# Cross attention on one core: the two big products by two levels of Winograd blocks in f32, or by three products of 12-bit parts

## The chip, the cores and the metric

The kernel runs on one core of a Trainium2 chip. The metric is the device time of one execution in microseconds, as the median of several runs. The profiled execution is one of its own; its span goes from the first to the last instruction and is a little shorter than the time of a run.

A core has five engines with a queue of instructions each, all in order: TensorE (matmuls, from SBUF into PSUM), VectorE, ScalarE, GpSimd and SyncE, which here only starts DMAs. GpSimd and ScalarE can start DMAs too. An instruction that waits holds everything behind it on its queue.

## The reference

Eight batches, 512 channels, 1024 positions. `x` are the inputs that ask, `ctx` those that are asked.

```python
q = einsum('bcn,dc->bnd', x, Wq) + bq           # 64 wide
k = einsum('bcn,dc->bdn', ctx, Wk) + bk[:, None]
v = einsum('bcn,dc->bdn', ctx, Wv) + bv[:, None]  # 512 wide
attn = softmax(einsum('bnd,bdm->bnm', q, k), axis=2)
out = einsum('bcm,bnm->bcn', v, attn) + x
```

All of it in float32. The two big products are V's (512 by 512 by 1024) and the last one (512 by 1024 by 1024).

## The kernel before, in words

A batch is done in this order: queries and keys (`project`, L181), scores in pairs of 64-row matmuls with the keys as columns on the partitions (`scores`, L223), the maximum over the keys (`fold`, `highest`; a reduction over partitions on GpSimd, L253), the exponentials E in place (`lower`, `exponential`), their sums (`total`, L258) and reciprocals. It never forms V. It takes Y = ctx E first and then Wv Y, so that Wv meets a matrix that is already summed, and divides Y by the sums in between (`scale_y`).

Both products go by Winograd's form of Strassen's scheme: a 2 by 2 block product with seven multiplications, and sums of blocks on both sides. In the first product the inputs' blocks `a` come from `x2T`, a transposed copy, and four of their sums (`S1` to `S4`) are made by VectorE, ScalarE and accumulating DMAs; the sums of E's blocks (`T1` to `T4`) by VectorE, ScalarE and DMAs. `multiply` (L375) does one of the seven products as two banks of four (first product) or two (second) matmuls 128 by 128 by 512. Five of the seven of the first product are split once more by the same scheme (`multiply_seeded`, `multiply_onto`, `inner_product` L437), with VectorE sums in `inner_left` and `inner_right`. Results are joined from PSUM by `evict_y` and `evict_o`.

The order of all engines is written out by hand (`manual_schedule`): `period` issues the instructions of a batch and, in between, scores, maxima and exponentials of the next batch and queries and keys of the one after. `head` is the special start of batch 0, with the loads of x1 and x2 in halves; the last batch adds x1 from SBUF and stores tile by tile. Elsewhere x1 is added to a result by an accumulating DMA on GpSimd's queue (L603) and the result is stored from SyncE's queue (L604).

All matmul operands are plain float32.

Of the kernel before, what the change touches and what calls it, by code (L numbers as in the profile page):

```python
# [9 lines left out]
F32 = mybir.dt.float32  # L10
AF = mybir.ActivationFunctionType
ALU = mybir.AluOpType


@with_exitstack
def kernel(
    ctx: ExitStack,
    tc: tile.TileContext,
    x1: bass.AP,
    x2: bass.AP,  # L20
    x2T: bass.AP,
# [4 lines left out]
    out: bass.AP,  # L26
):

    nc = tc.nc
    P = 128
    B, C, N = x1.shape
    D = wqk.shape[3]
    CT = C // P
    H = 512
    MH = N // P // 2  # L70
    WARM = 12
# [4 lines left out]
    dram = ctx.enter_context(  # L76
        tc.tile_pool(name="dram", bufs=2, space=bass.MemoryType.DRAM)
    )
    ps_s = ctx.enter_context(
        tc.tile_pool(name="ps_s", bufs=2, space=bass.MemoryType.PSUM)  # L80
    )
    ps_a = ctx.enter_context(
        tc.tile_pool(name="ps_a", bufs=1, space=bass.MemoryType.PSUM)
    )
# [3 lines left out]
    wq_sb, wk_sb = wqk_sb[:, 0], wqk_sb[:, 1]  # L88
    bq_sb, bk_sb = bqk_sb[:, 0:1], bqk_sb[:, 1:2]
    bv_sb = const.tile([P, CT], F32, name="bv_sb")  # L90
    w = {
        k: const.tile([P, 2, C // 2], F32, name=f"w_{k}")
        for k in ("11", "12", "21", "22", "S1", "S2", "S4")
    }

    def load_values():
        for r in range(2):
            for k in range(2):
                nc.sync.dma_start(w[f"{r + 1}{k + 1}"], wvT[r, k])

    def left_sums(a, *ks):

        for k in ks:
            if k == "S3":
                nc.vector.tensor_tensor(a["21"], a["11"], a["21"], ALU.subtract)
                a["S3"] = a["21"]
            elif k == "S4":
                nc.vector.scalar_tensor_tensor(a[k], a["12"], -1.0, a["S2"], ALU.mult, ALU.subtract)
            else:
                x, y, op = {"S1": ("21", "22", ALU.add), "S2": ("11", "S1", ALU.subtract)}[k]  # L110
                nc.vector.tensor_tensor(a[k], a[x], a[y], op)

    def value_sums(*ks):

        for k in ks:
            out, x, y, op = {
                "S1": ("S1", "21", "22", ALU.add),
                "S2": ("S2", "S1", "11", ALU.subtract),
                "S3": ("21", "11", "21", ALU.subtract),
                "S4": ("S4", "12", "S2", ALU.subtract),  # L120
            }[k]
            nc.vector.tensor_tensor(w[out], w[x], w[y], op)
        w["S3"] = w["21"]

    class Batch:
        def __init__(self, b):
            self.b = b
            self.a, self.e, self.t, self.y, self.o = {}, {}, {}, {}, {}
            self.mx, self.top, self.den, self.few, self.rden, self.row = {}, {}, {}, {}, {}, {}
            self.tmp, self.bank = {}, {}  # L130
            self.inner = {}

    def load_x(s, x):

        s.x = sb.tile([P, CT, N], F32, tag="x", name=f"x_{s.b}_{x.tensor.name}")
        for c in range(CT):
            nc.sync.dma_start(s.x[:, c, :], x[s.b, ts(c, P), :])

    def load_a(s, *ks):
        for k in ks:  # L140
            s.a[k] = sb.tile(
                [P, MH, C // 2], F32, tag=f"a{k}", name=f"a{k}_{s.b}", bufs=1 + (k[0] == "2")
            )
            nc.sync.dma_start(s.a[k], x2T[s.b, int(k[0]) - 1, int(k[1]) - 1])

    def sum_a(s, *ks):
        for k in ks:
            if k != "S3":
                s.a[k] = sb.tile([P, MH, C // 2], F32, tag=f"a{k}", name=f"a{k}_{s.b}")
        left_sums(s.a, *ks)  # L150

    def begin_s1(s):

        s.a["S1"] = sb.tile([P, MH, C // 2], F32, tag="aS1", name=f"aS1_{s.b}")
        nc.sync.dma_start(s.a["S1"], x2T[s.b, 1, 0])

    def end_s1(s):

        nc.gpsimd.dma_start(s.a["S1"], x2T[s.b, 1, 1], accum_op=ALU.add)

    def negate(s, k):

        if k == "S2":
            s.a[k] = sb.tile([P, MH, C // 2], F32, tag="aS2", name=f"aS2_{s.b}")
        else:
            s.a[k] = s.a["21"]
        nc.scalar.mul(s.a[k], s.a["S1" if k == "S2" else "21"], -1.0)

    def add_11(s, k):

        nc.gpsimd.dma_start(s.a[k], x2T[s.b, 0, 0], accum_op=ALU.add)

    def project(s, nm, w_sb, bank=None):

        if bank:
            ps = ps_a.tile([P, H], F32, tag=bank, name=f"ps_{nm}_{s.b}")
        else:
            ps = ps_s.tile([P, 2, H], F32, tag="sc", name=f"ps_{nm}_{s.b}")[:, 0, :]
        for c in range(CT):
            for h, r in ((0, lo), (1, hi)):  # L180
                nc.tensor.matmul(  # L181
                    ps[r, :],
                    w_sb[:, c, :],
                    s.x[:, c, ts(h, H)],
                    start=(c == 0),
                    stop=(c == CT - 1),
                )
        return ps

    def queries(s, bank=None):  # L190

        ps = project(s, "q", wq_sb, bank)
        s.q = sb.tile([P, N], F32, tag="q", name=f"q_{s.b}", bufs=2)
        for h, r, o in ((0, lo, hi), (1, hi, lo)):
            nc.scalar.activation(
                s.q[r, ts(h, H)], ps[r, :], AF.Identity, bias=bq_sb[r, :]
            )
        for h, r, o in ((0, lo, hi), (1, hi, lo)):
            nc.sync.dma_start(s.q[o, ts(h, H)], s.q[r, ts(h, H)])

    def keys(s, bank=None):

        ps = project(s, "k", wk_sb, bank)
        s.k = sb.tile([P, H], F32, tag="k", name=f"k_{s.b}", bufs=2)
        nc.scalar.activation(s.k, ps, AF.Identity, bias=bk_sb)

    def scores(s, h, i, bank=None):


        if i == 0:  # L210
            s.e[h] = sb.tile([P, 2, MH, H], F32, tag=f"e{h}", name=f"e_{s.b}_{h}")
        e = s.e[h]
        if bank:
            whole = None
            ps = [
                ps_a.tile([P, H], F32, tag=f"{bank}{g}", name=f"ps_s{bank}{g}_{s.b}_{h}_{i}")
                for g in range(2)
            ]
        else:
            whole = ps_s.tile([P, 2, H], F32, tag="sc", name=f"ps_s_{s.b}_{h}_{i}")  # L220
            ps = [whole[:, g, :] for g in range(2)]
        for g, r in ((0, lo), (1, hi)):
            nc.tensor.matmul(  # L223
                ps[g], s.k[r, ts(i, P)], s.q[r, ts(h, H)], start=True, stop=True
            )

        def copy():
            if bank:
                for g in range(2):
                    nc.scalar.copy(e[:, g, i, :], ps[g])  # L230
            else:
                nc.scalar.copy(e[:, :, i, :], whole)  # L232

        copy.ps = ps
        return copy

    def fold(s, h, i, kind, op):

        e = s.e[h]
        if i == 1:  # L240
            s.mx[h] = sb.tile([P, 2, H], F32, tag="fold", name=f"{kind}_{s.b}_{h}", bufs=2)
        f = s.mx[h]
        nc.vector.tensor_tensor(f, e[:, :, 0, :] if i == 1 else f, e[:, :, i, :], op)  # L243

    def fold_halves(s, h, op):
        f = s.mx[h]
        nc.vector.tensor_tensor(f[:, 0, :], f[:, 0, :], f[:, 1, :], op)

    def highest(s, h, halves=True):
        if halves:  # L250
            fold_halves(s, h, ALU.max)
        s.top[h] = sb.tile([P, H], F32, tag="top", name=f"top_{s.b}_{h}", bufs=2)
        nc.gpsimd.partition_all_reduce(s.top[h], s.mx[h][:, 0, :], P, ReduceOp.max)  # L253

    def total(s, h):
        fold_halves(s, h, ALU.add)
        s.den[h] = sb.tile([P, H], F32, tag="den", name=f"den_{s.b}_{h}", bufs=2)
        nc.gpsimd.partition_all_reduce(s.den[h], s.mx[h][:, 0, :], P, ReduceOp.add)  # L258
        s.few[h] = sb.tile([P, H // P], F32, tag="few", name=f"few_{s.b}_{h}", bufs=2)
        nc.gpsimd.dma_start(  # L260
            s.few[h], s.den[h][0:1, :].rearrange("o (p f) -> o p f", p=P)
        )

    def invert(s, h):

        nc.vector.reciprocal(s.few[h], s.few[h])  # L266
        s.row[h] = row = dram.tile([1, H], F32, tag="row", name=f"row_{s.b}_{h}")
        nc.gpsimd.dma_start(row.rearrange("o (p f) -> (o p) f", p=P), s.few[h])

    def spread(s, h):  # L270

        s.rden[h] = s.den[h]
        nc.gpsimd.dma_start(s.rden[h], s.row[h].broadcast_to([P, H]))

    def shares(s, h):
# [761 lines left out]
```

## Time and profile before

| | us |
|---|---|
| median of 3 runs | 687.22 |
| lowest, highest run | 686.67, 687.75 |
| span of the profiled execution | 685.4 |
| TensorE busy | 677.5 |
| VectorE busy | 605.9 |
| ScalarE busy | 329.0 |
| GpSimd busy | 211.4 |

How to read the lines that follow: a group of instructions has its line in the kernel, its engine (PE is TensorE's matmuls, PEld its loads of the stationary operand, DVE VectorE, ACT ScalarE, POOL GpSimd, SP SyncE; a q behind a name is the queue that starts DMAs), the operation, the tiles written and read, shape and count; then busy microseconds and the mean nanoseconds of one; then idle time in front of it and what ended it. A row of the timeline has its start, its length, and the instructions that are merged in it. Matmuls overlap in their records: the pace is the distance of starts, not the length. A DMA row ends with the KB of one and the median microseconds from issue to landing.

### The profile page before, as it was taken

What the parts mean: (1) busy time and instruction counts of PE and PEld (TensorE: products, weight loads), DVE (VectorE), ACT (ScalarE), POOL (GpSimd) and SP (SyncE); (2) the same over time, 40 slices, a digit from 0 to 9 for tenths busy, and PEclk for the clock granted to TensorE, in tenths of its full rate; (3) what the DMA queues carried; (4) which work ended last, traced back from release to release, by engine and by line L of the source; (5) the groups of instructions that cost most, each with busy time, mean ns of one, the idle gap of its engine ahead of it and who ended that gap; (6) DMA issues with size and microseconds to landing.
All of it is one profiled execution on the core that took longest, in us unless ns stands there. A gap on an engine that the chain in (4) does not pass through costs nothing.

```text
span 685.4 us, 7053 instructions
## 1 busy us (share of the span) xinstructions
PE 677.5 (99%) x2384; PEld 391.1 (57%) x2384; DVE 605.9 (88%) x744; ACT 329.0 (48%) x545; POOL 211.4 (31%) x175
## 2 busy tenths in 40 slices
PE   8999999999999999999999999999999999999997
PEld 5333554535547665566655576464854747556763
DVE  1999997987799989799979999799999979999884
ACT  2734364236355465554645637446465356553320
POOL 0125113421153411633125421344214351364100
PEclk9999999999999999999999999999999999999999
DMA  9655366836958949889598795987969881689502
GB/s 300 267 212 172 139 231 120 201 105 187 248 143 194 198 155 266 193 186 218 160 291 160 187 240 143 298 166 180 253 135 214 177 202 64 125 155 269 128 14 109
DMA packets 49620, 126.89 MB, mean 185 GB/s; under 512 B 5424, under 2 KB 7728, under 8 KB 49584
## 3 DMA queue, kind: packets, MB, share of 16 engines
q0 software_dynamic: 21456, 50.93, 42.0%
q1 hardware_dynamic: 27840, 75.11, 29.9%
q10 hardware_dynamic: 288, 0.39, 0.2%
q8 instruction: 19, 0.31, 0.2%
q14 instruction: 17, 0.14, 0.1%
HBM read 85.20 MB, written 16.81 MB: 149 GB/s over the span
## 4 chain that ended last, share of the span: by engine, by line
PE 83%; DVE 8%; DMA 6%; issue 1%; ACT 1%; SPq 1%; DVEq 0%; ACTq 0%; POOLq 0%
PE ps_ya L375 13%; PE ps_oa L375 9%; PE ps_yc L437 7%; PE ps_oc L375 7%; PE ps_ya L437 6%; PE ps_s L223 5%; PE ps_q L181 4%; PE ps_k L181 3%; PE ps_o L375 3%; PE ps_o L395 3%; PE ps_i3chain L437 3%; PE ps_i4chain L437 3%; PE ps_i7chain L437 2%; PE ps_i2chain L437 2%; DMA sum<-e 2%; PE ps_yc L375 2%
## 5 line engine op out<-in xcount | busy, mean ns | idle before, releaser
L375 PE MATMUL ps_ya<-eT,aS 128*128 128x512 f32 x192 | 84.9, 595 | 0.2 <-ACT uy L386 0.2
L258 POOL PARTITION_ALL_REDUCE den<-sum x16 | 53.5, 3345 | 96.4 <-DVE few L266 54.6
L288 DVE TENSOR_TENSOR e<-e,top 128x1024 f32<-128x1024 f32 x60 | 69.8, 1219 | 12.6 <-POOL top L253 12.6
L253 POOL PARTITION_ALL_REDUCE top<-max x16 | 38.0, 2376 | 98.5 <-DVE few L266 37.0
L292 ACT ACTIVATE e<-e 128x1024 f32<-128x1024 f32 x60 | 62.5, 1057 | 10.6 <-DVE e L288 9.1
L607 POOL DMA_DIRECT2D sum<-e x21 | 25.7, 1223 | 127.5 <-ACT sum L612 40.0
L375 PEld LDWEIGHTS ps_ya<-eT,aS 128*128 128x128 f32 x192 | 36.1, 190 | 44.8 <-issue 41.6
L375 PE MATMUL ps_oc<-yT,w 128*128 128x512 f32 x128 | 57.5, 593 | 0.5 <-DVE uo L600 0.5
L375 PE MATMUL ps_oa<-yT,w_S 128*128 128x512 f32 x128 | 57.6, 593 | 0.0
L232 ACT COPY e<-ps_s 128x1024 f32<-128x1024 f32 x46 | 45.4, 1027 | 12.5 <-PE ps_s L223 12.0
L223 PE MATMUL ps_s<-q,k 64*128 64x512 f32 x188 | 49.0, 608 | 0.8 <-ACT q L642 0.8
L386 ACT COPY uy<-ps_ya 128x512 f32<-128x512 f32 x28 | 16.0, 589 | 55.1 <-PE ps_ya L375 48.6
L375 PEld LDWEIGHTS ps_oc<-yT,w 128*128 128x128 f32 x128 | 24.2, 190 | 31.5 <-issue 29.2
L375 PEld LDWEIGHTS ps_oa<-yT,w_S 128*128 128x128 f32 x128 | 24.2, 190 | 30.8 <-issue 30.1
L243 DVE TENSOR_TENSOR max<-max,e 128x1024 f32<-128x1024 f32 x30 | 36.7, 1225 | 2.2
L386 ACT COPY uo<-ps_oa 128x512 f32<-128x512 f32 x32 | 18.7, 585 | 37.0 <-PE ps_oa L375 37.0
L223 PEld LDWEIGHTS ps_s<-q,k 64*128 64x128 f32 x188 | 17.9, 186 | 23.9 <-issue 18.3
L542 DVE TENSOR_TENSOR y<-y,den 128x1024 f32<-128x1024 f32 x24 | 29.3, 1221 | 0.3
L375 PE MATMUL ps_oa<-y,w_S 128*128 128x512 f32 (+1 forms) x68 | 28.8, 567 | 0.0
L395 PE MATMUL ps_o<-y,w 128*128 128x512 f32 x64 | 28.8, 592 | 0.0
L375 PE MATMUL ps_o<-y,w 128*128 128x512 f32 x64 | 28.8, 592 | 0.0
L551 DVE TENSOR_TENSOR y<-ps_yc,uy 128x512 f32<-128x512 f32 x40 | 25.7, 683 | 1.3 <-ACT uy L532 0.4
(200 smaller groups left out, 1475.5 us busy)
## 6 DMA issues: line engine op xcount, KB each, us to landing
x_in_x_dram<-in_x_dram SPq DMA_DIRECT2D x60, 512.0 KB, 7.6
a<-in_x2T_dram SPq DMA_DIRECT2D x32, 512.0 KB, 9.3
sum<-e POOLq DMA_DIRECT2D x21, 512.0 KB, 6.3
r<-in_x_dram POOLq DMA_DIRECT2D x14, 512.0 KB, 8.9
uo<-in_x_dram POOLq DMA_DIRECT2D x14, 512.0 KB, 8.5
out_dram<-r SPq DMA_DIRECT2D x14, 512.0 KB, 4.4
out_dram<-uo SPq DMA_DIRECT2D x14, 512.0 KB, 5.4
aS<-in_x2T_dram POOLq DMA_DIRECT2D x12, 512.0 KB, 6.4
```

Source lines behind the costliest of these rows:

```text
L181: nc.tensor.matmul(ps[r, :], w_sb[:, c, :], s.x[:, c, ts(h, H)], start=(c == 0), stop=(c == CT - 1),)
L223: nc.tensor.matmul(ps[g], s.k[r, ts(i, P)], s.q[r, ts(h, H)], start=True, stop=True)
L232: nc.scalar.copy(e[:, :, i, :], whole)
L243: nc.vector.tensor_tensor(f, e[:, :, 0, :] if i == 1 else f, e[:, :, i, :], op)
L253: nc.gpsimd.partition_all_reduce(s.top[h], s.mx[h][:, 0, :], P, ReduceOp.max)
L258: nc.gpsimd.partition_all_reduce(s.den[h], s.mx[h][:, 0, :], P, ReduceOp.add)
L288: nc.vector.tensor_tensor(e, e, top, ALU.subtract)
L292: nc.scalar.activation(e, e, AF.Exp)
L375: nc.tensor.matmul(ps[:, n], left[ka][:, k, ts(j, P)], right[kb][:, k, n], start=opens and k == 0, stop=i in (2, 3, 4) and k == n_k - 1, s ...
L386: nc.scalar.copy(s.tmp[i][:, j, :], ps)
L395: nc.tensor.matmul(ps, w["11"][:, k, ts(j, P)], s.y["11"][:, k, :], start=k == 0, stop=False, skip_group_check=True)
L437: nc.tensor.matmul(ps, s.inner[i][ka][:, k, :], s.inner[i, "t"][kb][:, k, :], start=opens and k == 0, stop=z in (2, 3, 4) and k == MH // 2 ...
```

## The change

The block scheme is gone. Every operand of the two big products is split into three parts of type float32r: `h`, the number rounded to 12 bits; `l`, the scaled or unscaled rest; `d`, a combination of both. Three matmuls (`d`, `h`, `l`) take the place of one, and the results X (from `h` and `l`) and Y (from `d`) are combined with factors of T = 4096 on the way out of PSUM.

V is now formed first, as [m, c] (`values`), with the bias already in Y's bank (`seed_y`); the last product takes E's columns as the stationary operand and V as the moving one, and gives the result as [n, c] (`results`), one tile of 128 positions by 512 channels at a time. The division by the sums has become the factor with which X and Y are taken out (`take_results`), since a position is now a partition. x1 comes a second time, transposed by the host (`x1T`), for the last addition by DMA; the host transposes the result back.

Work on E goes by units of 128 positions (`lower`, `exponential`, `high`, `rests`: 128 by 1024 elements each), scores, maxima and sums by quarters of 256 positions. The sum over the keys is a copy of one half of the quarter (ScalarE), an accumulating DMA of the other half, a reduction over partitions of 1024 columns, a DMA of one row to DRAM and two DMAs that lay the row down a column.

The period has two parts: `later_values` (eight tiles of V, with the first half of E's units in between) and `all_results` (eight tiles of the result, with the second half of E's units, and of the next batch: queries, keys, the first scores and the split of `ctx`). `first_values` takes the place of the first part in batch 0, and the new `head` loads ctx (2 MB), Wv (1 MB) and x (2 MB) in this order on SyncE's queue, splits the first chunk of ctx (`chunk`) and then Wv (`split_weights`: two ScalarE and two VectorE operations for each half), and makes the keys; `first_values` then issues queries, scores, maxima and units 0 to 3 between the eight tiles of V. As before, each half of q goes to the other 64 partitions by a DMA. `es`, `den` and the fold of the maxima have one buffer each, result tiles `o` four, PSUM's X and Y three banks each and the scores one tile of two banks. The ring for descriptors of GpSimd's DMAs is set to 8192 bytes.

```diff
-        "x2T": _np.asarray(ctx_2048).reshape(8, 2, 256, 2, 4, 128).transpose(0, 1, 3, 5, 4, 2),
+        "x1T": _np.asarray(x).transpose(0, 2, 1),
...
+T = 4096.0
+SPLIT = 1.0 - 2.0**-13
...
+    def high(s, u):
+        e = unit(s, u)
+        s.e[u] = {"h": half_of("h", [P, MT, P], f"e{s.b}_{u}")}
+        nc.scalar.activation(s.e[u]["h"], e, AF.Copy, scale=SPLIT)
+
+    def rests(s, u):
...
+        nc.vector.tensor_tensor(k["l"], e, f32(k["h"]), ALU.subtract)
+        nc.vector.scalar_tensor_tensor(k["d"], f32(k["l"]), -T, f32(k["h"]), ALU.mult, ALU.add)
+
+    def begin_sum(s, Q):
+        s.es[Q] = sb.tile([P, 4, QN], F32, tag="es", name=f"es_{s.b}_{Q}")
+        nc.scalar.copy(s.es[Q], s.raw[Q][:, 0:4, :])
+        nc.gpsimd.dma_start(s.es[Q], s.raw[Q][:, 4:8, :], accum_op=ALU.add)
+
+    def total(s, Q):
+        den = sb.tile([P, 4 * QN], F32, tag="den", name=f"den_{s.b}_{Q}")
+        nc.gpsimd.partition_all_reduce(den, s.es[Q].rearrange("p g n -> p (g n)"), P, ReduceOp.add)
+        row = dram.tile([1, 4 * QN], F32, tag="row", name=f"row_{s.b}_{Q}")
+        nc.sync.dma_start(row, den[0:1, :])
...
+            for t in range(2):
+                nc.sync.dma_start(few[:, t, :], row.rearrange("o (g t p) -> t p (o g)", g=4, t=2)[t])
...
+    def chunk(s, k):
...
+        nc.scalar.activation(p["h"], src, AF.Copy, scale=SPLIT)
...
+            nc.vector.tensor_tensor(p["l"], src, f32(p["h"]), ALU.subtract)
+            nc.vector.scalar_tensor_tensor(p["d"], f32(p["l"]), -T, f32(p["h"]), ALU.mult, ALU.add)
...
+    def seed_y(s, j):
+        s.Y[j] = ps_a.tile([P, C], F32, tag="Y", name=f"ps_vY_{s.b}_{j}")
+        nc.scalar.copy(s.Y[j], seed)
+
+    def values(s, j):
...
+        for z, ps in (("d", s.Y[j]), ("h", s.X[j]), ("l", s.X[j])):
+            for c in range(CT):
+                nc.tensor.matmul(
+                    ps, k[z][:, c, cols], w[z][:, c, :], start=(z == "h" and c == 0),
+                    stop=(z != "h" and c == CT - 1), skip_group_check=True,
+                )
...
+    def join_values(s, j):
...
+        nc.vector.scalar_tensor_tensor(s.v4[j // 2][:, j % 2, :], s.X[j], T + 1.0, s.y[j], ALU.mult, ALU.subtract)
+
+    def high_values(s, p):
...
+        nc.scalar.activation(s.v[p]["h"], s.v4[p], AF.Copy, scale=SPLIT / T)
+
+    def rest_values(s, p):
+        v = s.v[p]
+        nc.vector.scalar_tensor_tensor(v["l"], f32(v["h"]), -T, s.v4[p], ALU.mult, ALU.add)
+        nc.vector.tensor_tensor(v["d"], f32(v["h"]), f32(v["l"]), ALU.subtract)
+
+    def results(s, u, hooks=None):
...
+        for m in range(MT):
+            v = s.v[m // 2]
+            for z, ps in (("d", Y), ("h", X), ("l", X)):
+                nc.tensor.matmul(
+                    ps, e[z][:, m, :], v[z][:, m % 2, :], start=(m == 0 and z != "l"),
+                    stop=(m == MT - 1 and z != "h"), skip_group_check=True,
+                )
+            if hooks and m in hooks:
+                hooks[m]()
...
+    def take_results(s, u):
+        r = s.r[u // 2]
...
+        nc.scalar.activation(y, s.Y[u], AF.Identity, scale=r[:, 2, u % 2 : u % 2 + 1])
...
+        nc.vector.scalar_tensor_tensor(o, s.X[u], r[:, 1, u % 2 : u % 2 + 1], y, ALU.mult, ALU.subtract)
+        nc.gpsimd.dma_start(o, x1T[s.b, ts(u, P), :], accum_op=ALU.add)
+        nc.sync.dma_start(outT[s.b, ts(u, P), :], o)
...
+    def later_values(s, n, p):
+        for j in range(MT):
+            values(s, j)
+            if j in (3, 5):
+                scores(s, 2, j // 2 - 1)
+            if j == 0:
+                take_results(p, MT - 1)
+                if n:
+                    load_x(n, x1, 0, 1)
+                lower(s, 1)
+                exponential(s, 0)
+                highest(s, 1)
+            else:
+                copy_values(s, j - 1)
+            if j in (3, 5, 7):
+                rest_values(s, j // 2 - 1)
+            if j:
+                join_values(s, j - 1)
+            if j + 2 < MT:
+                seed_y(s, j + 2)
+            if j in (2, 4, 6):
+                high_values(s, j // 2 - 1)
+            if j == 1:
+                exponential(s, 1)
+                high(s, 0)
+            if j == 2:
+                high(s, 1)
+                rests(s, 0)
+            if j == 3:
+                begin_sum(s, 0)
+                lower(s, 2)
+            if j == 4:
+                exponential(s, 2)
+                rests(s, 1)
+            if j == 5:
+                high(s, 2)
+                lower(s, 3)
+                total(s, 0)
+            if j == 6:
+                exponential(s, 3)
+                highest(s, 2)
+            if j == 7:
+                begin_sum(s, 1)
+                scores(s, 3, 0)
+        take_values(s, MT - 1)
+        high_values(s, 3)
+
+    def all_results(s, n):
+        for u in range(MT):
...
+            if u + 4 < MT:
+                lower(s, u + 4)
+            if u == 0:
+                rest_values(s, 3)
+            results(s, u, hooks)
+            if n and u == 1:
+                load_x(n, x2, 0, 1)
+            if u % 2 == 1 and u < 7:
+                total(s, u // 2 + 1)
+            if u:
+                take_results(s, u - 1)
+            if 0 < u + 3 < MT:
+                high(s, u + 3)
+            if u + 4 < MT:
+                exponential(s, u + 4)
+            if u + 2 < MT:
+                rests(s, u + 2)
+            if n and u >= 4:
+                chunk(n, u - 4)()
+            if u == int(first):
+                highest(s, 3)
+            if n and u == 6:
+                highest(n, 0)
+            if n and u == 7:
+                seed_y(n, 0)
+                seed_y(n, 1)
+                lower(n, 0)
+            if u in (1, 3):
+                begin_sum(s, u // 2 + 2)
+            if u % 2 == 0:
+                shares(s, u // 2)
```

The hooks of `all_results` put these matmuls between those of a result tile (later batches): scores of the last quarter at tile 0 (behind m=3), the next batch's queries at tile 1, its keys at tile 4, its first scores at tiles 5 (two groups), 6 and 7.

More of the change, by code (lines that the diff above doesn't have):

```diff
@@ L181, in project @@
                 nc.tensor.matmul(
[L182 to L186, printed above, removed]
-                )
-        return ps
[L190 to L197, printed above, removed]
+                    ps[r, :], wqk_sb[:, which, c, :], x(h, c), start=(c == 0), stop=(c == CT - 1)
+                )
@@ L255, in total @@
[L255 to L268, printed above, removed]
@@ L1002 @@
+    states = [Batch(b) for b in range(B)] + [None]
     with tc.manual_schedule():
```

959 lines of the change are left out of this document (205 added, 754 removed).

## The prediction

> **What bounds the kernel now.** I read the page's totals first, then the chain that ended last, then one middle batch in a view by stretches of time.
>
> ```profile
> span 685.4 us, 7053 instructions
> PE 677.5 (99%) x2384; PEld 391.1 (57%) x2384; DVE 605.9 (88%) x744; ACT 329.0 (48%) x545; POOL 211.4 (31%) x175
> ...
> PE 83%; DVE 8%; DMA 6%; issue 1%; ACT 1%; SPq 1%; DVEq 0%; ACTq 0%; POOLq 0%
> ```
> ```profile
> core 0: us, PE busy (x) PEld busy (x) DVE busy (x) ACT busy (x) POOL busy (x), PEclk, DMA share, GB/s
> ...
> 285.00:367.00 82.00, 81.53 (x302) 49.58 (x300) 75.20 (x98) 42.76 (x73) 27.19 (x25) 1.00 0.85 207
> ```
>
> TensorE is fed without a gap at full clock (column PEclk) and carries the chain. Nothing else decides today, though VectorE is close behind with 75 of 82 us. So the change pays only in TensorE time, and only while VectorE does not become the bound. The timeline gives the pace:
>
> ```profile
> 116.56 3.60 PE L375 MATMUL ps_oc<-yT,w 128*128 128x512 f32 x8
> 119.99 7.03 PE L375 MATMUL ps_ya<-e,a 128*128 128x512 f32 x16
> ```
> ```profile
> 204.45 1.03 PE L437 MATMUL ps_i1chain<-e,a 128*128 128x256 f32 x4
> 205.31 1.03 PE L437 MATMUL ps_i1third<-eI1yT,aI 128*128 128x256 f32 x4
> ```
> ```profile
> 287.01 1.03 PE L437 MATMUL ps_i1chain<-e,a 128*128 128x256 f32 x4
> ```
>
> Eight records take 119.99 - 116.56 = 3.43 us, 0.429 each; every matmul of the program leaves two records. Four 256-column records take 0.86, 0.216 each. Two batches start at 204.45 and 287.01: a batch is 82.56 us. The first one has ended by 119.99.
>
> **The change part by part: TensorE.** An f32 matmul of 512 columns costs 2 x 0.429 = 0.86 us. If that is four passes, a single pass of 512 columns costs 0.215; no row shows the new operand type. The nearest row is the 256-column record: 0.216, with a 128x128 load of its own in front of each. Below: 0.215. Above: a whole 0.429. I take 0.216. Whether a load hides behind so short a matmul is shown by the load's own group, and the rest of TensorE's work by the chain:
>
> ```profile
> L437 PEld LDWEIGHTS ps_i1chain<-eI1yT,aI 128*128 128x128 f32 x48 | 9.1, 189 | 1.3
> ```
> ```profile
> 308.05 1.72 PE ps_s L223 x8
> 309.76 3.58 PE ps_q L181 x16
> ```
>
> 48 loads of 189 ns at that pace left 1.3 us idle in all, so they hide. Per batch the new kernel issues 8 x 12 single passes for V and 8 x 24 for the result, 288 x 0.216 = 62.2; queries and keys stay f32, 2 x 3.58 = 7.2; the 32 half-wide score matmuls are 8 x 0.86 = 6.9. Sum 76.3 us against 82.56. Left alone, that is 50 us off over eight batches.
>
> **VectorE.** The Winograd sums go; splitting comes in. Prices:
>
> ```profile
> L288 DVE TENSOR_TENSOR e<-e,top 128x1024 f32<-128x1024 f32 x60 | 69.8, 1219 | 12.6 <-POOL top L253 12.6
> ```
> ```profile
> L600 DVE SCALAR_TENSOR_TENSOR uo<-ps_oc,bv_sb,uo 128x512 f32<-128x512 f32 x28 | 19.7, 744 | 3.6 <-ACT e L292 2.6 <-PE ps_oc L375 1.0
> ```
> ```profile
> L247 DVE TENSOR_TENSOR max<-max 128x512 f32<-128x512 f32 x16 | 11.1, 691 | 0.5
> ```
> ```profile
> L266 DVE RECIPROCAL few<-few 128x4 f32<-128x4 f32 x16 | 2.7, 170 | 1.7 <-DMA few<-den 1.7
> ```
>
> Per batch: 44 operations of 1024 columns (16 in `rests`, 8 in `chunk`, 8 in `rest_values`, 8 `lower`, 4 in `highest`) x 1.219 = 53.6; 16 on PSUM (`join_values`, `take_results`) x 0.744 = 11.9; the tails of `highest`, 4 x (0.69 + about 0.42) = 4.4; 16 small ones in `shares` x 0.17 = 2.7. Sum 72.6 us of 76.3. That would fit if it were spread evenly. It is not: I walked the order of the engines through one later batch, from the moment TensorE starts its first V matmul (0).
>
> TensorE asks for the last quarter of V (`vd3`, matmul m=6 of the first result tile) after 96 V matmuls (20.7), four groups of scores (3.4) and 18 result matmuls (3.9): at 28.1. In VectorE's queue up to `rest_values(3)` stand 18 operations of 1024 columns, 9 on PSUM and two `highest` tails. Back to back they are a little closer than their durations:
>
> ```profile
> 361.09 4.63 DVE L288 TENSOR_TENSOR e<-e,top 128x1024 f32<-128x1024 f32 x4 [4.34 <-POOL top L253]
> ```
> ```profile
> 365.64 0.69 DVE L247 TENSOR_TENSOR sum<-sum 128x512 f32<-128x512 f32 x1
> 366.24 1.41 DVE L600 SCALAR_TENSOR_TENSOR uo<-ps_oc,bv_sb,uo 128x512 f32<-128x512 f32 x2
> 366.43 3.23 POOL L258 PARTITION_ALL_REDUCE den<-sum  x1 [4.26 <-DVE sum L247]
> ```
> ```profile
> 367.56 2.18 DVE L426 TENSOR_TENSOR eI1yT<-e 128x1024 f32<-128x1024 f32 x1
> ```
>
> (365.64 - 361.09)/4 = 1.14 and (367.56 - 366.24)/2 = 0.66, so 18 x 1.14 + 9 x 0.66 + 2.2, and some 0.1 more for each of 8 that read the operation before them, is 29.5. It starts at 0.8, after ScalarE's copy of the old batch's last Y (0.585, and an estimated 0.2 to hand over): 30.3 with no wait at all. Three waits for ScalarE add 2.9: `copy_values(1)` stands behind the exponentials (0.6); the score copy issued at j=3 waits in ScalarE's queue until TensorE has done V tile 3, and `copy_values(2)` behind it holds `join_values(2)` (1.1); `copy_values(7)` stands behind `begin_sum(1)` and another score copy (1.2). ScalarE's prices for this:
>
> ```profile
> L292 ACT ACTIVATE e<-e 128x1024 f32<-128x1024 f32 x60 | 62.5, 1057 | 10.6 <-DVE e L288 9.1
> ```
> ```profile
> L386 ACT COPY uo<-ps_oa 128x512 f32<-128x512 f32 x32 | 18.7, 585 | 37.0 <-PE ps_oa L375 37.0
> ```
>
> In all ScalarE has 28 wide ones (29.6) and 24 of 512 columns (14.0) and the projections' 2: about 46 us plus 8 score copies, 54. It is not full, only in the way. Last, the operation at 367.56 took 2.18 us while GpSimd's reduction ran, against 1.22 for its like:
>
> ```profile
> L426 DVE TENSOR_TENSOR eI4eT<-eT 128x1024 f32<-128x1024 f32 x8 | 9.7, 1218 | 0.0
> ```
>
> One such reduction costs VectorE about 1 us; `total(0)`, twice as wide, falls into just this stretch. Bounds 0 and 3; I take 1.5. So `vd3` is there at 30.3 + 2.9 + 1.5 = 34.7 and TensorE stands 6.6 us. From then on TensorE has 46.9 us of work to VectorE's 43 and VectorE catches up, so the loss is paid once a batch: period 76.3 + 6.6 = 82.9. Ends: 78.5 (no waits, no contention), 88 (next paragraph).
>
> **GpSimd and its DMAs.** `es` and `den` have one buffer each, so the four sums of a batch run in a row: copy, accumulating DMA, reduction, next copy.
>
> ```profile
> L258 POOL PARTITION_ALL_REDUCE den<-sum x16 | 53.5, 3345 | 96.4 <-DVE few L266 54.6 <-DVE sum L247 41.7
> L253 POOL PARTITION_ALL_REDUCE top<-max x16 | 38.0, 2376 | 98.5 <-DVE few L266 37.0 <-DVE max L247 34.9 <-DVE max L720 18.4
> ```
> ```profile
> sum<-e POOLq DMA_DIRECT2D x21, 512.0 KB, 6.3
> ```
> ```profile
> few<-den POOLq DMA_DIRECT2D x16, 2.0 KB, 2.0
> row<-few POOLq DMA_DIRECT2D x16, 2.0 KB, 3.7
> ```
>
> The rows are for 512 columns; `total` now reduces 1024, `highest` 256. Bounds for `total`: 3.3 (all fixed) and 6.7 (all by column). I take 6.0 and 1.5, since adding and taking the maximum over the same shape differ by 1 us, so most of it is work per column. `highest(3)` is behind `vd3` in VectorE's queue: done at 39.5. Reductions: `top(3)` to 41, `total(1)` to 47; copy 48, landing 54.3, `total(2)` 60.3; copy 61.3, landing 67.6, `total(3)` 73.6; row and column DMAs (SP's queue, where the loads stand ahead) 5.7: 79.3. TensorE's batch ends at 82.9: 3.6 us to spare, so I add nothing. The DMA engines are no new bound: a batch now moves 10 MB (2 each of x, ctx, x again and result, 0.5 for each sum), where the window above had a share of 0.85 at 207 GB/s for 17. On GpSimd's queue the accumulating DMA of a result tile stands behind `total`, which waits for its sum to land; a tile is stored late by that, but four `o` buffers cover it, and only `take_results(7)` of the last batch is on the path.
>
> **Head and tail.**
>
> ```profile
> 6.17 3.65 PE L638 MATMUL ps_q<-x_head,wqk_sb 128*64 128x512 f32 x16 [0.55 <-DMA x_head<-in_x_dram]
> ```
> ```profile
> 9.63 1.93 PE L653 MATMUL ps_kc<-x_head,wqk_sb 128*64 128x256 f32 x16
> ```
> ```profile
> uo<-in_x_dram POOLq DMA_DIRECT2D x14, 512.0 KB, 8.5
> ```
> ```profile
> q<-q SPq DMA_DIRECT2D x14, 128.0 KB, 4.5
> out_dram<-x_in_x_dram SPq DMA_DIRECT2D x7, 256.0 KB, 2.1
> ```
>
> The first MB lands by 6.2, the next 3.5 later. The new head needs 2 MB of ctx and 1 MB of Wv (13.2), then four ScalarE and two VectorE steps to split Wv: V starts at 21. In batch 0 nothing has run ahead: three more `chunk`s come first on VectorE (28), queries wait for the q DMA (scores at 38), the maxima follow at 44, 63 and 77 (the last behind `begin_sum(1)`, which waits for `total(0)`), and `vd3` is ready at 82. Then 1.3 + 46.9: batch 0 ends at 131 against 120 now. VectorE's own 45 us after 21 would give 114; I keep 114 to 138. The last batch: 34.7 + 1.3 + 7 x 5.18 = 72.3, then copy, combine, an accumulating DMA of half the 8.5 row's size (about 6.5) and the store (2.1), 10: 82.
>
> **Sum.** 131 + 6 x 82.9 + 82 = 710 against the span of 685.4. The median of the runs is 1.8 above the span (687.22), so 712.
>
> **The rivals.** *VectorE keeps ahead (faster).* If ScalarE's score copies do not hold the joins and the reductions do not disturb, the period is 78.5 and the head nearer 118: 118 + 6 x 78.5 + 77 + 2 = 668. It turns at a period of 78.7, where 131 + 6P + 82 meets 685.4. For it: the 72.6 us fit into 76.3. Against: even waitless, `vd3` comes 2 us late.
>
> *The sums close the ring (slower still).* If `total` takes 8 us or the landing 8.5, the three steps grow by 6, shares come at 85, `take_results(6)` and the bias seeds behind it hold the next batch's first V matmul: period 87, 131 + 522 + 95 + 2 = 750. For it: the chain is serial. Against: 3.6 us to spare.
>
> *The weight load shows, or the single pass is none.* Each single pass then costs 0.216 + 0.19, or 0.429: period 131 or 138, time 1080 or more. Against it stand the 48 loads above. The Trainium skill ("TensorE: Matmul & The Clock Gate", Part 3) says that LDWEIGHTS overlaps running matmuls only where the row group differs; that rule would give this case, and the rows above, all of 128 rows, disagree with it.
>
> *The reductions shut VectorE out.* If every reduction (4 x 6 + 4 x 1.5 = 30 us a batch) stopped VectorE altogether, its queue would be 103 us long: 8 x 103 + 45 = 870. The Trainium skill ("SBUF — State Buffer", Who interferes with whom) has a VectorE instruction with two SBUF inputs and a GpSimd one that reads SBUF block each other for the whole instruction; the row of 2.18 us beside a reduction of 3.23 shows a loss of 1 us, not of 3.
>
> **How the numbers follow.** Chances: the sum above 0.50, the ring 0.18, the load 0.04, the shut-out 0.04, VectorE ahead 0.22, a tie 0.02. A measurement of this kernel tells 0.2% (1.4 us) from no change. Faster 0.22, same 0.02, slower 0.76. The likeliest case alone spans 690 to 735. The range reaches 668 to 758: it holds the ring and the better half of the faster case and leaves out the two dear rivals and the tails, together less than 0.2.
>
> **What would show it.** Single-pass records 0.216 apart with their loads hidden (TensorE's part); in each later batch a TensorE gap of about 6 us in front of m=6 of the first result tile, released by VectorE's `vd3` (the walk); `total` at 6 us (the ring); batch 0 ending near 131. The forecast is wrong if that gap is under 3 us, if TensorE is found standing at the batch's first V matmul for `seed_y`, or if the passes are not 0.216.

## The result, and the profile after

The changed kernel takes 826.5 us (median of 4 runs, 824.6 to 830.3) against 686.9 (4 runs): 1.204 times as long (95% interval 1.201 to 1.207). The forecast was 712, with a range of 668 to 758. The sign was right, the size was not. The four runs differ as TensorE's granted clock does: 824.6 us at a mean clock of 0.951, 830.3 at 0.939; the profile is of the longest.

The page of the changed kernel, its totals, TensorE's granted clock in 40 slices, and the chain that ended last:

```profile
span 828.5 us, 8390 instructions
PE 714.5 (86%) x3078; PEld 510.3 (62%) x3078; DVE 652.7 (79%) x677; ACT 412.1 (50%) x511; POOL 339.3 (41%) x166
...
PEclk9897799998998999998998999999999999999987
...
DVE 14%; PE 13%; issue 8%; POOL 6%; DMA 4%; ACT 3%; SPq 0%; POOLq 0%; DVEq 0%; ACTq 0%
```

Before, TensorE carried 83% of the chain and was busy for 99%. Now it stands idle for 14% of a longer span, and it is also busy for longer: 714.5 us against 677.5, where the forecast's stream of 76.3 a batch would have made some 610. No single engine carries the chain. The clock falls below full again and again; before it did not.

One middle batch, from its first V matmul to the next batch's, in four stretches: V, first result tile, the other seven, wait for the next batch. Columns as in the same view of before: time, then busy us of TensorE, its loads, VectorE, ScalarE and GpSimd with their instruction counts, granted clock, DMA share and GB/s.

```profile
445.70:473.89 28.19, 28.19 (x120) 21.76 (x121) 24.61 (x23) 18.44 (x25) 8.60 (x5) 0.90 0.49 131
473.89:488.20 14.31, 8.61 (x34) 6.03 (x33) 14.14 (x15) 8.68 (x10) 4.42 (x3) 0.90 0.24 38
488.20:539.50 51.30, 51.30 (x233) 35.93 (x232) 38.35 (x43) 21.40 (x25) 27.86 (x12) 1.00 0.56 124
539.50:542.96 3.46, 0.08 (x2) 0.00 (x1) 2.38 (x7) 2.17 (x4) 1.48 (x2) 1.00 0.19 76
```

And TensorE's timeline at the gaps (start, length, what, and in brackets the idle time before it and who ended it):

```profile
445.70 2.08 PE L200 MATMUL ps_vY<-wd,kd_x 128*128 128x512 f32 x4 [3.41 <-ACT ps_vY L193]
...
475.78 0.50 PE L232 MATMUL ps_oX<-vh,kh_e 128*128 128x512 f32 x1 [1.39 <-DVE v L212]
480.15 1.13 PE L110 MATMUL ps_s<-q,k 64*128 64x256 f32 x8 [1.58 <-ACT e L115]
485.60 0.80 PE L232 MATMUL ps_oY<-vd,kd_e 128*128 128x512 f32 x1 [2.73 <-DVE vd L221]
486.19 0.63 PE L232 MATMUL ps_oX<-vh,kh_e 128*128 128x512 f32 x1
486.62 0.63 PE L232 MATMUL ps_oX<-vl,kl_e 128*128 128x512 f32 x1
```

The batch is 97.26 us; over six middle batches (153.38 to 729.76) the mean is 96.1. TensorE stands 3.41 us at the batch's first V matmul, for the bias seed (L193), and 5.7 us in three pieces in the first result tile. Behind the last of these, passes start 0.43 apart (486.19, 486.62): half speed. The first stretch has it too, with a clock of 0.90.

Not every batch has it. In the last of the six TensorE waits in the same four places (8.2 us in all), and the passes behind the same wait for `vd3` keep their pace; the whole batch runs at full clock:

```profile
674.20 0.50 PE L232 MATMUL ps_oY<-vd,kd_e 128*128 128x512 f32 x1 [2.73 <-DVE vd L221]
674.54 0.40 PE L232 MATMUL ps_oX<-vh,kh_e 128*128 128x512 f32 x1
674.78 0.40 PE L232 MATMUL ps_oX<-vl,kl_e 128*128 128x512 f32 x1
```
```profile
636.85:729.76 92.91, 84.17 (x385) 60.75 (x385) 80.76 (x85) 50.71 (x64) 42.53 (x21) 1.00 0.50 117
```

Four of the six batches have half speed both at their start and in the first result tile and take 96.8 to 97.8 us, the fifth only at its start (93.9), the sixth not at all (92.9).

What VectorE and GpSimd do in the same batch, first in the V phase, then among the results:

```profile
468.63 7.00 POOL L160 PARTITION_ALL_REDUCE den<-es  x1 [3.77 <-DMA es<-e]
469.57 0.68 DVE L212 SCALAR_TENSOR_TENSOR v<-ps_vX,vy 128x512 f32<-128x512 f32 x1
470.17 4.96 DVE L132 TENSOR_TENSOR e<-e,top 128x1024 f32<-128x1024 f32 x1
```
```profile
508.57 6.11 POOL L160 PARTITION_ALL_REDUCE den<-es  x1 [6.28 <-DMA es<-e]
...
510.28 0.16 DVE L171 TENSOR_REDUCE r<-few 128x2 f32<-128x8 f32 x1 [7.08 <-DMA few<-row]
510.67 2.45 DVE L173 TENSOR_SCALAR r<-r 128x2 f32<-128x2 f32 x1
...
522.70 7.01 POOL L160 PARTITION_ALL_REDUCE den<-es  x1 [2.59 <-DMA es<-e]
...
524.04 4.12 DVE L173 TENSOR_SCALAR r<-r 128x2 f32<-128x2 f32 x1
...
539.81 0.15 DVE L171 TENSOR_REDUCE r<-few 128x2 f32<-128x8 f32 x1
```

An operation of 1.2 us takes 4.96 while the sum is reduced; one of two columns takes 2.45 and 4.12. VectorE is stopped for 2.3 to 4 us. It also stood 7.08 us for the row of the second sum. The last shares of the batch come at 539.81; nothing but VectorE's own queue ended their wait, and the seed follows them through ScalarE.

### The profile page after: what moved, and what is told of

Same layout as the page of the kernel before. It is cut to its first block, busy times and chain, and to the rows that moved or that the text cites. A ratio compares the mean times of both kernels' runs of the same rounds, so it can differ in the third digit from the quotient of the medians.

```text
span 828.5 us, 8390 instructions
## 1 busy us (share of the span) xinstructions
PE 714.5 (86%) x3078; PEld 510.3 (62%) x3078; DVE 652.7 (79%) x677; ACT 412.1 (50%) x511; POOL 339.3 (41%) x166
## 5 line engine op out<-in xcount | busy, mean ns | idle before, releaser
L160 POOL PARTITION_ALL_REDUCE den<-es x32 | 213.2, 6661 | 89.8 <-DMA es<-e 89.8
L232 PE MATMUL ps_oY<-vd,kd_e 128*128 128x512 f32 x512 | 214.0, 418 | 32.8 <-DVE vd L221 27.2
L232 PE MATMUL ps_oX<-vh,kh_e 128*128 128x512 f32 x512 | 206.2, 403 | 9.7 <-DVE v L212 9.7
L232 PE MATMUL ps_oX<-vl,kl_e 128*128 128x512 f32 x512 | 204.8, 400 | 0.0
L232 PEld LDWEIGHTS ps_oY<-vd,kd_e 128*128 128x128 f32 x512 | 99.5, 194 | 83.5 <-DVE vd L221 30.8
L232 PEld LDWEIGHTS ps_oX<-vh,kh_e 128*128 128x128 f32 x512 | 99.9, 195 | 30.6 <-DVE v L212 11.9
L232 PEld LDWEIGHTS ps_oX<-vl,kl_e 128*128 128x128 f32 x512 | 99.5, 194 | 21.9
L200 PE MATMUL ps_vY<-wd,kd_x 128*128 128x512 f32 x256 | 76.9, 424 | 28.8 <-ACT ps_vY L193 28.1
L151 DVE SCALAR_TENSOR_TENSOR kd_e<-kl_e,kh_e 128x1024 fp32r<-128x1024 f32 x64 | 82.9, 1296 | 2.2
L150 DVE TENSOR_TENSOR kl_e<-e,kh_e 128x1024 fp32r<-128x1024 f32 x64 | 84.1, 1314 | 0.0
```

The lines of the kernel that those rows point to most:

```text
L150: nc.vector.tensor_tensor(k["l"], e, f32(k["h"]), ALU.subtract)
L151: nc.vector.scalar_tensor_tensor(k["d"], f32(k["l"]), -T, f32(k["h"]), ALU.mult, ALU.add)
L160: nc.gpsimd.partition_all_reduce(den, s.es[Q].rearrange("p g n -> p (g n)"), P, ReduceOp.add)
L200: nc.tensor.matmul(ps, k[z][:, c, cols], w[z][:, c, :], start=(z == "h" and c == 0), stop=(z != "h" and c == CT - 1), skip_group_check=True,)
L232: nc.tensor.matmul(ps, e[z][:, m, :], v[z][:, m % 2, :], start=(m == 0 and z != "l"), stop=(m == MT - 1 and z != "h"), skip_group_check=True,)
```

## The experiments

Each is the changed kernel with one edit, or TensorE's part alone. In some a part of the computation is left out, as their expectations say, so their times are those of less work. Periods are means over the six middle batches; the changed kernel's is 96.1.

**TensorE alone.** All other work is left out: no splits, no sums, no loads of x; two batches of matmuls in the order of the kernel on fixed tiles, then stretches of one kind (one profiled run; the clock is full throughout the two batches).

> Only TensorE's instructions, on fixed tiles: two whole batches in the changed kernel's order, then stretches of one kind each; softmax, splitting, evictions and loads are left out. If a single pass of the new type and each change of kind cost TensorE more than I reckoned, whoever waits for what, a batch takes 82 to 83 us here too and a single pass 0.227. If TensorE's pace in the changed kernel was stretched by the other engines, a batch takes 76.3 us and a pass 0.216.

TensorE's timeline, the first group of scores in each of the two batches:

```profile
25.02 0.70 PE L73 MATMUL ps_S<-q 64*128 64x256 f32 x4
...
108.21 1.13 PE L73 MATMUL ps_S<-q 64*128 64x256 f32 x8
```

108.21 - 25.02 = 83.19 us a batch with nothing to wait for, where the sum had 76.3. That is already more than a whole batch of before (82.56). Single passes come 0.227 apart, in one bank or six in rotation, with a new stationary tile each or the same one, which is loaded again each time; the f32 records of 256 columns come 0.216 apart.

**What the difference is made of.** More stretches of TensorE alone.

> TensorE's instructions alone on fixed tiles; the computation itself is left out. Stretches: 144 single passes of 512 columns; 288 of 256; 48 groups of four f32 256-column matmuls on all rows and one pass; 48 of four f32 matmuls on rows 0 to 63 and one pass; 48 of four f32 matmuls on row halves in turn; 48 of two f32 on all rows and two on a half; 48 of four f32 on all rows and four passes; last, stretches of 96 passes parted by a wait for 1 to 6 copies of ScalarE in a row. Pace: if the 11 ns above 0.216 are paid by the instruction, the 256-column passes come 0.119 apart, if by the column 0.113. Change of kind: if the 0.20 us belongs to the operand type, it shows wherever f32 and single passes alternate (four f32 and a pass: 0.86 + 0.23 + 0.2 = 1.29), whether f32 uses all rows or half; if it belongs to the row groups, it is absent with all rows (1.09) and present where f32 on all rows and on a half alternate. Waits: theory 'a wait of about 3 us halves the clock for some us, a shorter one does not': passes at 0.43 behind the longer waits alone; rival 'every wait does it': behind each of the six.

TensorE's timeline: four f32 matmuls on all rows alternating with four passes, then two f32 matmuls on all rows alternating with two on rows 0 to 63 (two records for each f32 matmul).

```profile
477.29 1.28 PE L65 MATMUL ps_X<-m,a 128*128 128x512 f32 x4
478.40 1.89 PE L68 MATMUL ps_X<-raw 128*128 128x256 f32 x8
479.94 0.81 PE L65 MATMUL ps_X<-m,a 128*128 128x512 f32 x2
```
```profile
339.45 1.13 PE L68 MATMUL ps_X<-raw 128*128 128x256 f32 x4
340.51 1.13 PE L72 MATMUL ps_S<-q 64*128 64x256 f32 x4
341.57 0.70 PE L68 MATMUL ps_X<-raw 128*128 128x256 f32 x2
```

Four f32 matmuls and four passes take 479.94 - 477.29 = 2.65 us; at their own paces they are 8 x 0.216 + 4 x 0.227 = 2.64. A change of operand type costs nothing that shows. Four f32 matmuls, two on all rows and two on half, take 2.12 against 1.73: 0.20 for each change between all rows and half of them. So my "kind" was the row set: the scores use 64 rows, all else 128. (The expectation's 0.86 for four f32 matmuls on all rows was a slip for 1.73.) The Trainium skill has this ("TensorEngine Tiling (Array Packing)", Key Properties: changing the tiling mode drains TensorE); it gives no price, the runs do.

Windows over the stretches of 512 and of 256 columns:

```profile
13.00:40.00 27.00, 27.00 (x119) 22.05 (x118) 0.00 (x0) 1.45 (x2) 0.00 (x0) 1.00 0.00 1
45.00:80.00 35.00, 35.00 (x290) 34.84 (x289) 0.00 (x0) 0.00 (x0) 0.00 (x0) 1.00 0.00 1
```

27 / 119 = 0.227 and 35 / 290 = 0.121: half the columns save 0.106, so about 15 ns of a pass do not go with its columns; whether they belong to the instruction or to its load was not parted. Of the 6.9 us that the stream was short, 288 x 0.011 = 3.1 are the passes and 8 groups x 2 x 0.20 = 3.2 the row sets; 0.6 is left, most of it at the two projections, which write half the columns of the array: the pass ahead of one starts 0.32 before it, and the first pass behind it 0.34 before the next.

The waits, TensorE's timeline of the third and fourth, each read in a window of about 4 us:

```profile
629.01 0.70 PE L118 MATMUL ps_S<-g 128*128 128x256 f32 x2 [2.03 <-ACT g L117]
629.36 2.88 PE L65 MATMUL ps_X<-m,a 128*128 128x512 f32 x11
```
```profile
654.18 0.70 PE L118 MATMUL ps_S<-g 128*128 128x256 f32 x2 [2.68 <-ACT g L117]
654.52 3.87 PE L65 MATMUL ps_X<-m,a 128*128 128x512 f32 x9
```

After 0.7, 1.4 and 2.0 us of idling the pace stays; after 2.7, 3.3 and 4.0 the passes fall to half speed within 1 us. In the kernels the length of the wait does not decide alone: the 2.73 us for `vd3` are followed by half speed in five of the changed kernel's seven later batches, and not in the other two.

**The row DMA ahead of the load.** In the batch above, the row of sums issued at 498.19 landed 7.6 us later, behind the load of x2; VectorE's 7.08 us end when the columns made from that row have landed.

```
-            if n and u == 1:
-                load_x(n, x2, 0, 1)
             if u % 2 == 1 and u < 7:
                 total(s, u // 2 + 1)
+            if n and u == 1:
+                load_x(n, x2, 0, 1)
```

> The 2 MB load of the next ctx is issued behind the first sum's row instead of ahead of it. If the ring of the four sums holds the bias seeds and with them the next batch, the row lands some 6 us sooner, the gap of 3.4 us at a batch's start and the half-speed matmuls after it go, and the time falls by 25 to 45 us, to 780 to 800. If the lock between GpSimd's reductions and VectorE sets the pace by itself, nothing changes by more than 5 us.

834.4 us, period 96.0: missed, neither case holds. VectorE now waits 2.84 for that row, but the load comes later, and with it the keys; the next reduction then meets a wide operation instead of a small one. The chain of waits:

```profile
497.43 11.98 DMA x_in_x_dram<-in_x_dram
509.46 3.66 PE ps_k L83 x14
...
517.51 5.57 DVE kl_x L186
```

What was saved at the row is lost to the keys and the stop. The late row was real, and not what decided.

**A narrow reduction.**

```
-        nc.gpsimd.partition_all_reduce(den, s.es[Q].rearrange("p g n -> p (g n)"), P, ReduceOp.add)
+        nc.gpsimd.partition_all_reduce(den, s.es[Q][:, 0, :], P, ReduceOp.add)
...
```

The tiles `den`, `row` and `few` shrink to a quarter with it.

> The sums' reduction takes 256 columns instead of 1024 (three quarters of the denominators are left out). The reduction falls from 6.7 to under 2 us, the ring is short and VectorE is hardly shut out. If the two together are what is lost beside TensorE's price, a batch comes to 84 to 87 us and the whole to 710 to 740. If only the ring counts, about 780; if the half-speed matmuls come from elsewhere, over 800.

761.8 us, period 88.8: 65 us gone, with GpSimd's 213 us of these reductions made into 74. It fell between the two expectations, and it alters two things: the stops, and the length of the ring. (The shorter row is no part of the gain: VectorE waits 50 us in all for its columns, and 51 in the changed kernel.) Two more kernels part them.

**The same length, narrow.** The edit: the narrow reduction stands in `for _ in range(3):`.

> Like e3_narrow (a sum reduced over 256 columns, three quarters of each denominator left out), but the same narrow reduction is made three times in a row, so GpSimd is busy for 3 x 2.3 = 6.9 us in each sum, as long as in the changed kernel. Theory 'the wide reduction stops VectorE': three narrow ones stop it by 0.8 us each at most, the sums are late again but VectorE's queue is not longer: period 89 to 91, 765 to 785. Rival 'the ring of sums is too long, whoever computes': the shares come as late as in the changed kernel, the seed waits again 3.4 us and the clock falls: period 95 to 97, 810 to 830.

781.8 us (1.138, 1.135 to 1.141), period 90.3. The page's totals and two groups:

```profile
PE 700.4 (90%) x3078; PEld 501.9 (64%) x3078; DVE 590.3 (76%) x677; ACT 412.4 (53%) x511; POOL 321.4 (41%) x230
...
L161 POOL PARTITION_ALL_REDUCE den<-es x96 | 196.3, 2045 | 98.6 <-DMA es<-e 92.7
L132 DVE TENSOR_TENSOR e<-e,top 128x1024 f32<-128x1024 f32 x64 | 81.9, 1280 | 2.4 <-POOL top L124 2.4
```

GpSimd works nearly as long as in the changed kernel (321 us against 339), VectorE's same 677 operations take 590.3 instead of 652.7, and 45 of the 65 us stay gone. The length of the ring is worth at most 20.

**The stop without the ring.** With the narrow reduction in `total`, and behind the accumulating DMA of a sum in `begin_sum`:

```
+        dump = sb.tile([P, 2, C], F32, tag="dump", name=f"dump_{s.b}_{Q}")
+        nc.gpsimd.partition_all_reduce(
+            dump.rearrange("p g n -> p (g n)"), f32(w["h"][:, 0:2, :]).rearrange("p g n -> p (g n)"), P, ReduceOp.add
+        )
```

> Like e3_narrow (three quarters of each denominator left out), and while the accumulating DMA of a sum is under way GpSimd makes a wide reduction of 1024 columns of a constant tile, whose result nobody reads. A sum then takes 6.9 + 2.3 from the issue of its DMA, where the changed kernel takes 5 to 6 + 6.8: the ring is shorter by 2 to 3 us for each sum, the wide reduction is as long as there. Theory 'the wide reduction stops VectorE': VectorE loses about 4 us for each again, period 93 to 97, 800 to 830. Rival 'the ring': the shares come nearly as early as in e3_narrow, period 89 to 91, 762 to 785.

862.4 us, period 100.5: more than the theory's 800 to 830, and far from the rival's.

```profile
PE 725.9 (84%) x3078; PEld 516.4 (60%) x3078; DVE 701.8 (82%) x677; ACT 414.2 (48%) x511; POOL 387.6 (45%) x198
...
L158 POOL PARTITION_ALL_REDUCE dump<-wh x32 | 204.7, 6397 | 0.0
L150 DVE TENSOR_TENSOR kl_e<-e,kh_e 128x1024 fp32r<-128x1024 f32 x64 | 158.6, 2478 | 0.0
```

The wide reduction of a tile that nobody waits for brings the loss back. It now falls beside `rests`, whose mean goes to 2.5 us, and VectorE's total rises by 130 us over the narrow kernel's 571.3. GpSimd's queue is also 6.4 us longer for each sum here, so not all 100 us are the stop.

**Fewer operations ahead of vd3.**

```
     def rests(s, u):
         e, k = unit(s, u), s.e[u]
+        if s.b and u < 2:
+            k["l"] = k["d"] = k["h"]
+            return
```

> Changed kernel, but in batches 1 to 7 the units 0 and 1 use their high part for all three passes: four VectorE operations of 1024 columns (4.9 us by the row of 1.22) are left out of the V phase, TensorE issues the same matmuls. Theory 'the first result tile stands because of the length of VectorE's queue': the three gaps of a batch in front of and inside the first result tile (1.4, 1.6, 2.7) go, and with them the half-speed passes behind them (about 2 us): 7.5 us in each of 7 batches, so 826 - 52 = about 774; a period of 89 to 91. Rival 'ScalarE's order or the sum makes vd3 late': vd3 is not earlier, the gaps stay, the time stays over 812.

824.3 us, period 95.5: missed, the rival holds. Of the three gaps the first falls from 1.4 to 0.5, the second stays at 1.6, and in front of m=6 TensorE stands as long as before:

```profile
479.03 0.57 PE L235 MATMUL ps_oY<-vd,kh_e 128*128 128x512 f32 x1 [2.72 <-DVE vd L224]
```

Taking 4.9 us out of VectorE's queue does not make `vd3` earlier. Here too a `lower` is stopped (4.81 us at 463.75), the join of V tile 5 behind it ends at 469.2, ScalarE's `high_values` has waited 4.00 for it, and behind that stand the exponential, a copy of `es`, a copy of scores and `copy_values(7)`. So the trace reads as a chain from engine to engine; no run changed ScalarE's order to test it.

**Both.** With the narrow reduction as well:

> e3_narrow and e5_no_rests together (three quarters of the denominators and the splits of units 0 and 1 of later batches left out), TensorE's instructions unchanged. Theory 'TensorE's own stream costs 83.2 us a batch whatever the others do': with no stall left the period falls from 88.8 to 83 to 84.5, the time to 761.8 - 7 x 5 = about 727, and no lower. Rival 'TensorE's stream is 76.3 and the rest hidden waits': the period falls below 81, the time below 705.

752.6 us (1.095, 1.093 to 1.097), period 87.6: only 9 less than narrow alone, not the 35 expected. 2.8 us of gaps stay in each batch (1.9 for `vd3`, 0.8 for the seed). The period never falls below 83.2. Two of the six batches run at full clock and take 86.6 us; in the other four half speed follows the wait for `vd3`, and they take 88.2.

**The sums folded on VectorE.** `begin_sum` becomes three VectorE additions down to 256 columns, in place of copy and DMA; the reduction is narrow and the whole result is computed.

> The whole sum is kept, but VectorE folds the eight blocks to one (2.3 us more for each quarter), so that ScalarE's copy and the accumulating DMA go and GpSimd reduces 256 columns. If the ring and the lock cost more than VectorE's 9.3 us a batch, it is faster than the changed kernel: 740 to 770. If VectorE's total sets the pace, it gives nothing or costs time: 820 to 850.

804.6 us, period 93.6: between both. The additions cost about 9 us of VectorE a batch (4 x (1.2 + 0.7 + 0.4)), nearly what the stops had.

**Four narrow ones.** The whole result is computed here too:

```
-        nc.gpsimd.partition_all_reduce(den, s.es[Q].rearrange("p g n -> p (g n)"), P, ReduceOp.add)
+        for g in range(4):
+            nc.gpsimd.partition_all_reduce(den[:, ts(g, QN)], s.es[Q][:, g, :], P, ReduceOp.add)
```

> The changed kernel with the whole computation; each reduction of 1024 columns is made as four of 256 into the four quarters of the same tile, 4 x 2.05 = 8.2 us by the row of e6_narrow_thrice, where the one took 6.7. Theory 'the wide form stops VectorE, its length does no harm': VectorE's wide operations keep their 1.2 to 1.3 us, period 90 to 93, 780 to 805, faster than the changed kernel by 20 to 45 although GpSimd works longer. Rival 'GpSimd's time is what counts': sums 1.5 us later each, four of them, 826 + 7 x 6 = 868, or at best 826.

805.8 us (1.172, 1.170 to 1.174), period 92.8: 21 us less than the changed kernel, though GpSimd is busy for longer, and level with the folded sums (804.6). The rival is out. The time lies just above the theory's 780 to 805, and not all wide operations keep 1.2 to 1.3 us, as short stops remain:

```profile
PE 701.7 (88%) x3078; PEld 503.6 (63%) x3078; DVE 617.8 (77%) x677; ACT 412.4 (51%) x511; POOL 386.3 (48%) x262
...
L161 POOL PARTITION_ALL_REDUCE den<-es x128 | 265.4, 2146 | 86.5 <-DMA es<-e 86.5
L151 DVE SCALAR_TENSOR_TENSOR kd_e<-kl_e,kh_e 128x1024 fp32r<-128x1024 f32 x64 | 97.3, 1521 | 2.2
```

VectorE's total is 35 us below the changed kernel's, but still some 46 above that of one narrow reduction for each sum (571.3).

## Why the prediction was wrong, point by point

The prediction's own sum against the measured starts, all in the profiled executions:

| part | forecast | measured |
|---|---|---|
| batch 0 ends | 131 | 153.4 |
| a middle batch | 82.9 | 96.1 |
| the last batch and the tail | 82 | 98.7 |
| span | 710 | 828.5 |

A middle batch of 96.1 is 83.2 of TensorE's own stream, 8.9 of gaps and 3.9 that are left over. Against the forecast: +6.9, +2.3, +3.9. In the batch at full clock 1.5 is left over (92.9 - 83.2 - 8.2), so some 2.4 of the 3.9 are half speed; the 1.5 were not traced further.

- **TensorE's stream: the term on which the gain rested was mis-sized.** "Sum 76.3 us against 82.56" took each pass at 0.216 and the scores at 0.86 a group as if they stood alone. Passes cost 0.227, which the prediction had named as a sign of being wrong, and each switch to the 64 rows of the scores and back 0.20. At 83.2 the new stream is no shorter than the old batch: the rival in which VectorE keeps ahead (668) could not happen, and stalls were all that was left to add. Even with the shortest batch 0 of these runs, that of the narrow reduction, no stall in the next six and the forecast's last, it would end at 143.7 + 6 x 83.2 + 82 = 725. That the loads hide was right, against the rule that the prediction cited.
- **The price of a reduction on VectorE: the step that set the size.** The prediction took 1.5 us once a batch, for `total(0)`, from a row of 512 columns that lost 1 us. At 1024 columns three of the four sums of the batch above stop an operation: 4.96 for 1.22, 2.45 and 4.12 for 0.17, together 10 us. The row of before was a mild one: in the same trace an operation of the same size took 3.26 us beside such a reduction (L301, at 59.80). With nothing but a narrower reduction VectorE's total fell by 81.4 us, 10.2 a batch. The 72.6 us of VectorE's own work were near: the narrow kernel has 571.3 / 8 = 71.4. The shut-out rival had the mechanism, but at 30 us a batch too dear: a third of that was lost.
- **The walk to vd3.** The first result tile has gaps of 5.7 us, for 6.6 forecast in front of m=6. That the sum is near is luck: it is three gaps, and the one in front of m=6 is 2.73, under the 3 us that the prediction had named as a sign of being wrong. Nor is it the length of VectorE's queue alone: four operations fewer take 0.9 off the first gap and nothing off the last. With the narrow reduction the first two gaps are gone and 2.62 stay in front of m=6; there four operations fewer take 0.7 off, and 1.9 stay. By the trace the rest is a hand-over between VectorE and ScalarE; that is argued, not tested.
- **The ring: "3.6 us to spare, so I add nothing" failed.** TensorE was found standing at the first V matmul for `seed_y`, 3.4 us in the batch above, which the prediction had named as what would refute it. `total` took 6.66 where I had 6.0, and one row 7.6 us to land; but what ends last is VectorE's queue, in which the last shares stand behind two stops and the 7 us wait. Three narrow reductions, as long in the ring, leave 0.8 to 1.4 us of this gap.
- **The clock was in no case.** Before, no gap of TensorE in the middle batches was longer than 0.6 us, and the clock stayed full. Here each batch has waits of 2.5 to 3.7 us at its start and 2.73 in the first result tile, and behind them the passes often, not always, run at half speed: in the batch above the first V tile takes 5.28 us for 2.72.
- **Batch 0**: V began at 21.96 (forecast 21), but `vd3` came at 90.9 instead of 82, and the gaps behind its first matmul add up to 26 us. The narrow reduction alone brings its end to 143.7, so 9.7 of the 22 us are the reductions. The rest was not parted; the dearer stream is in it.
- **The last batch** has the waits of the others and one more of 3.7 us for E's `kd`, gaps of 12.5 us in all. Its 98.7 for 82 were not parted further.

## What to carry to other kernels

Before a stream of matmuls is priced by one row, let it run alone in its real order: the pace of the new form and the switches between row sets ate the whole gain here, and one kernel without any waits shows it. An engine's busy time is not its own: compare it between kernels with the same instructions, and look for single operations of several times their usual length beside a reduction on GpSimd. Where TensorE idles in pieces, allow for half speed behind each piece as well, and try several narrow reductions for one wide one: here four of 256 columns took 21 us less than one of 1024, though each still stops VectorE a little.

## What the runs showed of the hardware that was not expected

- A wide reduction across partitions can stop VectorE for more than half of its length, and its price grows with the width: of 6.7 us at 1024 columns up to about 4 are lost, of 3.3 at 512 mostly about 1 and up to 2.0, and at 256 (2.0 to 2.3) a wide operation took up to 2.12 for 1.22. The Trainium skill ("SBUF — State Buffer", Who interferes with whom) has such a pair block each other for the whole instruction; here VectorE loses a part of it. Two-column operations with a single input are stopped too (4.12 us).
- Single passes of the new operand type come 0.227 apart at 512 columns and 0.121 at 256, so about 15 ns of each do not go with its columns. The f32 records show nearly none of that: 0.429 at 512 columns and 0.216 at 256.
- Half speed can follow a TensorE wait, and the length of the wait alone does not tell whether it does. In TensorE alone 2.03 us left the pace and 2.68 halved it. In the kernels 1.9 us were followed by half speed in four of seven batches (narrow reduction and fewer operations), 2.73 in five of seven (the changed kernel), and 3.65 were not (the row ahead of the load, at 155.94).
